# Four graph layers on one core: the chain from a third-layer unit to the last layer's products, re-cut

## The chip, the cores and the metric

One core of a Trainium2 chip. The metric is the device time of one execution in microseconds, the median over runs of the same kernel. An execution of the kernel before takes 1645.74 us (1645.39 to 1646.08 over 3 runs); the profiled one has a span of 1643.8 us.

## The reference, cut to what matters

Eight batch elements with 2048 nodes and 64 features pass through four layers. Each layer adds its input and is followed by a layer norm. All share one adjacency matrix.

```python
x = _layernorm(x + _L0_gnn_ref(x, adj, ...), axis=-1)   # attention, layer norm inside, elu
x = _layernorm(x + _L1_gnn_ref(x, ..., adj), axis=-1)   # attention, elu
x = _layernorm(x + _L2_gnn_ref(x, adj, ...), axis=-1)   # attention, relu
x = _layernorm(x + _L3_gnn_ref(x, ..., adj), axis=-1)   # below

# layer 2, the "third layer"
h = jnp.matmul(x, W)
e = leaky_relu(f1[:, :, None] + f2[:, None, :])         # f1, f2: h times the two halves of a
attention = softmax(where(adj > 0, e, NEG_BIG), axis=2)
out = relu(matmul(attention, h))

# layer 3, the last layer
feat = softplus(x * (INV_SQRT2 * w0) + b0)
scores = feat * wa + ba
attn = softmax(where(mask, scores[:, None, :, :], -1e9), axis=2)
out = einsum('bijd,bjd->bid', attn, feat)
```

In the last layer the score of a neighbour depends on the neighbour and the feature alone. So with v = exp(scores) the output of a node is the sum over its neighbours of feat*v divided by the sum of v: two products of the adjacency matrix with a 2048 x 64 matrix for each element. A node without neighbours gets the mean of feat.

## The kernel before, in words

**Units.** The first three layers are done in 24 units of (layer, element): elements 0 to 3 through layers 0 and 1, then 4 to 7 through both, then layer 2 for elements 0 to 7. A unit is a loop over 16 steps, one for each block of 128 neighbours (`attend`, L899). In layer 2 a step is: POOL clamps a 128x2048 tile w from a row that is spread over the partitions (`clamp`, two steps ahead), ACT takes the exponential of each half of it into a PSUM tile e (`exponential`, one step ahead), DVE multiplies each half by the adjacency matrix (`edge`, fp8) back into w, and PE multiplies w with x into two accumulator banks (four products in the program, eight in the profile).

**Streams.** All other work is written as generators that a list of streams (`Streams`, L1190) advances by one pause at each attention step: `yield n` means "go on n steps later". Every engine executes its queue in the order in which these steps put instructions there. So the number and the place of the pauses decide where in an engine's queue an operation stands. After a unit's 16th step a chain of streams is added: `finish` (L937: divide, residual, statistics, normalize), then `scores` for the next layer or, after layer 2, `l3_features`. `group` (L757) makes the row maxima that layer 2 needs for four elements at a time; it runs once after element 3 and once after element 7 of layer 1.

**Banks.** [...] two for the accumulators of the running unit, two "side" banks (`pm`), handed out by a counter `pm_slots`, and four more that the current layer uses in its own way (in layer 2, two tiles e of two banks each). `Banks.share()` (L120) takes one of the two side banks away for the last layer's products (`pl_slots`). It is called at the hand-over to the first unit of layer 2, although the products begin only when the first two elements are through it. With one side bank, `finish` and `transposed` fetch one bank at a time instead of two (`Banks.width`).

**The last layer.** Its products need more than bf16 precision, so each operand is cut into three bf16 pieces v0, v1, v2 that add up to the fp32 value. `l3_features` (L1048) does, for one element: softplus (Abs, Exp, Ln, Relu on ACT, an addition on DVE), the scores on POOL, the sum of the features (`fs`) on DVE, the exponential, feat*v, then the pieces: ACT casts to v0, POOL subtracts it from the fp32 value, ACT casts the rest to v1, POOL subtracts again into v2. In between PE turns `fs` into a mean over all nodes (`p_fm`, `q.fm`), on which the stream waits for a side bank. Two elements make a pair with shared piece tiles 128 x 16 x 256; there are four pairs, and all but the last share one set of piece tiles (`v_slots`), so a pair's pieces are made when the pair before has placed all its products. The products of a pair (`l3_products`, L1115) are 16 row blocks of 48 matmuls (16 neighbour blocks by three pieces, `edge` stationary, 256 columns moving), placed as half blocks of 24, one per attention step when pieces and a bank are there. ACT copies a row block out (`nd`), and for every two row blocks `l3_finish` (L1158) divides, adds, normalizes and stores. When the eight units of layer 2 are over, the streams run alone until everything is placed (`now[0]` is 3); products then use the banks of the tiles e, which are two row blocks.

The profile gives nearly every instruction the line L78, that of the recording helper, so its groups are told apart by tile names: `acc` and `w` are attention, `p_l` the last layer's products, `vf` the fp32 value, `v` the pieces, `nd` the copied products, `st`, `isw` and `sq` statistics.

Of the kernel before, what the change touches and what calls it, by code (L numbers as in the profile page):

```python
# [8 lines left out]
F32 = mybir.dt.float32  # L9
# [5 lines left out]
ALU = mybir.AluOpType  # L15
AX = mybir.AxisListType

P = 128
# [30 lines left out]
def gnn4_kernel(ctx: ExitStack, tc: tile.TileContext, t, out):  # L49
    nc = tc.nc  # L50
    x_in, adjT = t["x"], t["adjT"]
    B, N, F = x_in.shape
# [9 lines left out]
    small = ctx.enter_context(tc.tile_pool(name="small", bufs=2))  # L62
# [40 lines left out]
    pm_slots = Slots(2)  # L103

    class Banks:
# [4 lines left out]
        pool = None  # L110
# [9 lines left out]
        @classmethod  # L120
        def share(cls):

            cls.shared = True
            pm_slots.n -= 1

        @classmethod
        def width(cls):
# [6 lines left out]
    xT_slots, h_slots, sq_slots, e_slots, v_slots, pl_slots, oT_slots = (  # L134
        Slots(1) for _ in range(7)
    )
    vf_slots, nd_slots, o_slots, lo_slots = (Slots(2) for _ in range(4))

    pe, dve, act, pool = (InOrder(e) for e in (nc.tensor, nc.vector, nc.scalar, nc.gpsimd))

    def psum(name):
        return pm.tile([P, 512], F32, tag="pm", name=name)
# [10 lines left out]
    ones = consts.tile([P, P], F32, name="ones")  # L153
# [67 lines left out]
    p = psum("p_nodes")  # L221
# [137 lines left out]
    def softplus(f, y, src):  # L359

        act.activation(y, src, AF.Abs, scale=l3c[:, 0:1], bias=l3c[:, 1:2])
        yield 1
        act.activation(y, y, AF.Exp, scale=-1.0)
        yield 1
        act.activation(y, y, AF.Ln, bias=1.0)
        yield 1
        act.activation(f, src, AF.Relu, scale=l3c[:, 0:1], bias=l3c[:, 1:2])
        yield 1
        dve.tensor_tensor(f, f, y, ALU.add)
# [387 lines left out]
    def group(gi):  # L757
# [61 lines left out]
        yield 1  # L819

        am = small.tile([P, NB, K], F32, tag="am", name=f"am_{nm}", bufs=1)
        slots = pl_slots if Banks.shared else pm_slots
        yield from slots.take()
        Banks.busy += 1
        p = psum(f"p_lse_{nm}")
        for ib in range(K):
            for jb in range(K):
                pe.matmul(
                    p[:, NB * ib : NB * (ib + 1)],
                    lhsT=edge[:, jb, ib * P : (ib + 1) * P],  # L830
                    rhs=te[:, jb, :],
                    start=(jb == 0),
                    stop=(jb == K - 1),
                )
            if ib % 4 == 3 or (gi == 0 and ib % 2):
                yield 1 if gi else 2
        dve.tensor_scalar(
            am.rearrange("p b k -> p k b"),
# [98 lines left out]
    def finish(u):  # L937
        layer, b = u.layer, u.b
        yield from oT_slots.take()
        oT = tmp.tile([P, 2, 512], F32, tag="oT", name=f"oT_{u.n}")  # L940
        for c in range(2):
            act.copy(oT[:, c], u.acc[c])
        if layer == 0:
            hb = early.tile([P, K, F], F32, tag="hb", name=f"hb_{u.n}", bufs=1)
            for sl, y in V[0, b].parts:
                pool.tensor_tensor(
                    hb[:, :, sl], y, bc_k(gamma[:, sl], K, y.shape[2]), ALU.mult
                )
        yield 1
        yield from o_slots.take()  # L950
        o = tmp.tile([P, K, F], F32, tag="o", name=f"o_{u.n}", bufs=2)
        o5 = o.rearrange("p (c h s) f -> p c s h f", c=2, h=2)
        done = 0
        while done < 4:
            width = Banks.width()
            ps = []
            yield from pm_slots.take(width)
            for i in range(done, min(done + width, 4)):
                c, s0 = i // 2, 2 * (i % 2)
                p = psum(f"p_o_{u.n}_{c}_{s0}")  # L960
                for s in range(2):
                    k = s0 + s
                    pe.matmul(
                        p[:, s * 2 * F1 : (s + 1) * 2 * F1],
                        lhsT=oT[:, c, k * P : (k + 1) * P],
                        rhs=RH[layer].rearrange("p h f -> p (h f)"),
                        start=True,
                        stop=True,
                    )
                ps.append((c, s0, p))  # L970
            done += width
            if done >= 4:
                oT_slots.give()
            yield 2 if pairs and width == 2 else 1
            for c, s0, p in ps:
                p4 = p[:, : 4 * F1].rearrange("p (s h f) -> p s h f", s=2, h=2)
                den = small.tile([P, 2, 2], F32, tag="den", name=f"den_{u.n}_{c}_{s0}")
                dve.reciprocal(den, p4[:, :, :, F])
                if layer == 2:
                    dve.tensor_tensor(  # L980
                        o5[:, c, s0 : s0 + 2],
                        p4[:, :, :, :F],
                        den[:, :, :, None].to_broadcast([P, 2, 2, F]),
                        ALU.mult,
                    )
                    continue
                for s in range(2):
                    for h in range(2):
                        act.activation(
                            o5[:, c, s0 + s, h],  # L990
                            p4[:, s, h, :F],
                            AF.Copy,
                            scale=den[:, s, h : h + 1],
                        )
            pm_slots.give(width)
        if layer == 2:
            for sl, x in x_cur[b].parts:
                dve.scalar_tensor_tensor(o[:, :, sl], o[:, :, sl], 0.0, x, ALU.max, ALU.add)
            yield 1
        else:  # L1000
            yield 1
            if layer == 0:
                pool.tensor_tensor(o, o, hb, ALU.add)
                yield 2

            yield from e_slots.take()
            e = tmp.tile([P, K, F], F32, tag="e", name=f"eh_{u.n}")
            act.activation(e, o, AF.Relu, scale=-1.0)
            act.activation(e, e, AF.Exp, scale=-1.0)
            yield 1  # L1010
            for sl, x in x_cur[b].parts:
                pool.tensor_tensor(
                    e[:, :, sl], e[:, :, sl], x, ALU.add
                )
            act.activation(o, o, AF.Relu)
            yield 1
            pool.tensor_tensor(o, o, e, ALU.add)
            e_slots.give()
            yield 1
        nm, rs = yield from stats(o, K, f"x_{u.n}")  # L1020
        xn = Rows(x_cur[b].t, layer < 2)
        if layer == 2:
            dve.tensor_tensor(o, o, bc_f(rs), ALU.mult)
            dve.tensor_tensor(xn.v, o, bc_f(nm), ALU.add)
            yield 1
        else:
            yield 1
            for k in range(K):
                act.activation(
                    xn.block(k), o[:, k], AF.Identity, scale=rs[:, k : k + 1], bias=nm[:, k : k + 1]  # L1030
                )
                if k % K2 == K2 - 1:
                    yield 1
            xn.settle()
        o_slots.give()
        x_cur[b] = xn
        V[layer + 1, b] = xn
        yield 1


    class Pair:
# [2 lines left out]
    pairs = []  # L1044

    now = [0]

    def l3_features(b):  # L1048

# [12 lines left out]
        y = tmp.tile([P, K, F], F32, tag="e", name=f"sp_{n}")  # L1062
        yield from softplus(f, y, x_cur[b].v)
        e_slots.give()
        yield 1
        v = late.tile([P, K, 2, F], F32, tag="vf", name=f"vf_{n}", bufs=2)
        pool.tensor_tensor(v[:, :, 1], f, bc_k(wa), ALU.mult)
        pool.tensor_tensor(v[:, :, 1], v[:, :, 1], bc_k(l3off), ALU.add)
        fs = small.tile([P, F], F32, tag="fs", name=f"fs_{n}")
        dve.tensor_reduce(fs, f.rearrange("p k f -> p f k"), AX.X, ALU.add)  # L1070
        yield 3
        act.activation(v[:, :, 1], v[:, :, 1], AF.Exp)
        yield 1
        dve.tensor_tensor(v[:, :, 0], f, v[:, :, 1], ALU.mult)
# [19 lines left out]
                yield 1  # L1094
        act.copy(q.v[0][:, :, i], v)
        yield 1
        pool.tensor_tensor(v, v, q.v[0][:, :, i], ALU.subtract)
        yield from pm_slots.take()
        p = psum(f"p_fm_{n}")
        pe.matmul(p[:, :F], lhsT=ones, rhs=fs, start=True, stop=True)  # L1100
        yield 1

        q.fm[i] = small.tile([P, F], F32, tag="fm", name=f"fm_{n}", bufs=4)
        dve.tensor_scalar(q.fm[i], p[:, :F], 1.0 / N, -1.0, ALU.mult, ALU.add)
        pm_slots.give()
        act.copy(q.v[1][:, :, i], v)
        yield 1
        pool.tensor_tensor(q.v[2][:, :, i], v, q.v[1][:, :, i], ALU.subtract)
        vf_slots.give()
        yield 1  # L1110
        q.ready += 1
# [2 lines left out]

    def l3_products():  # L1115

        for m in range(B // 2):
            while len(pairs) <= m or pairs[m].ready < 2:
                yield 1
            q = pairs[m]  # L1120
            for ib in range(K):
# [143 lines left out]
    for n, (layer, b) in enumerate(todo):  # L1265
# [17 lines left out]
        def handover():  # L1283

            if not done or nxt is None or S[nxt].__dict__.get("begun"):
                return
            if in_psum(*nxt):
                if n == 0:
                    Banks.use("psR", 1)
                spread(*nxt)  # L1290
            elif nxt == (2, 0):
                Banks.use("psE", 2)
                Banks.share()
            S[nxt].begun = True
            first_exponentials()

# [546 lines left out]
```

## Time and profile before

| | us | share of the span |
|---|---|---|
| span | 1643.8 | |
| PE, matmuls | 1349.0 | 82% |
| DVE | 1301.1 | 79% |
| POOL | 823.7 | 50% |
| ACT | 802.8 | 49% |
| PE, products of the last layer (`p_l`, 3072) | 351.1 | |
| layer 2, units 0 to 7 | 838.1 to 1396.5 | 34% |
| after the last unit | 1396.5 to 1643.8 | 15% |

A row of groups gives the operation, the tiles written and read with their shapes, its count, then busy time, the mean of one in ns, and the idle time of the engine just before it with what ended it. A row of windows gives, for a stretch of time, how long each engine was busy and with how many instructions. The chain of waits is followed back from the last instruction: each line is a start, a length, and the engine and tile that the end of the program waited for at that time.

### The profile page before, as it was taken

What the parts mean: (1) busy time and instruction counts of PE and PEld (TensorE: products, weight loads), DVE (VectorE), ACT (ScalarE), POOL (GpSimd) and SP (SyncE); (2) the same over time, 40 slices, a digit from 0 to 9 for tenths busy, and PEclk for the clock granted to TensorE, in tenths of its full rate; (3) what the DMA queues carried; (4) which work ended last, traced back from release to release, by engine and by line L of the source; (5) the groups of instructions that cost most, each with busy time, mean ns of one, the idle gap of its engine ahead of it and who ended that gap; (6) DMA issues with size and microseconds to landing.
All of it is one profiled execution on the core that took longest, in us unless ns stands there. A gap on an engine that the chain in (4) does not pass through costs nothing.

```text
span 1643.8 us, 20952 instructions
## 1 busy us (share of the span) xinstructions
PE 1349.0 (82%) x8162; PEld 667.2 (41%) x8162; DVE 1301.1 (79%) x1334; ACT 802.8 (49%) x1635; POOL 823.7 (50%) x726
## 2 busy tenths in 40 slices
PE   3687879888888898888887676699896999587996
PEld 2222323333333343233322231165452545476885
DVE  4888877899887989898888878969897977738444
ACT  5234664443265443442378857676656664242111
POOL 2145353422222454321257748877789877546332
PEclk9999988899998999999999878899998999888998
DMA  8800000000000000000000000000010000000000
GB/s 329 215 5 1 1 2 1 1 2 1 1 1 2 1 2 2 2 1 26 26 1 26 26 1 27 0 26 8 30 33 7 4 4 11 10 4 14 11 14 19
DMA packets 42190, 36.86 MB, mean 22 GB/s; under 512 B 37509, under 2 KB 37813, under 8 KB 39906
## 3 DMA queue, kind: packets, MB, share of 16 engines
q1 hardware_dynamic: 41538, 34.26, 6.8%
q8 instruction: 66, 1.08, 0.3%
q10 hardware_dynamic: 544, 1.17, 0.2%
q14 instruction: 42, 0.34, 0.1%
HBM read 30.94 MB, written 4.45 MB: 22 GB/s over the span
## 4 chain that ended last, share of the span: by engine, by line
PE 31%; DVE 17%; ACT 7%; POOL 4%; issue 3%; POOLq 0%; DVEq 0%; ACTq 0%
PE p_l L78 18%; PE acc L78 11%; DVE w L78 10%; ACT e L78 3%; DVE o L78 2%; DVE st_x L78 2%; DVE x L78 1%; POOL v L78 1%; PE p_o L78 1%; ACT x L78 1%; POOL vf L78 1%; DVE f L78 1%; PE p_s L78 1%; POOL w L78 1%; POOL o L78 1%
## 5 line engine op out<-in xcount | busy, mean ns | idle before, releaser
L78 PE MATMUL acc<-w,pv 128*64 128x512 f32 x2048 | 525.4, 642 | 117.0 <-DVE w L78 95.1
L78 DVE SCALAR_TENSOR_TENSOR w<-r,se,edge 128x2048 f32<-128x2048 f32 x240 | 551.9, 2340 | 27.1 <-PE r L78 26.3
L78 PEld LDWEIGHTS <-edge 128*128 128x128 fp8e4 x3842 | 321.2, 99 | 153.1 <-issue 94.3
L78 PE MATMUL p_l<-v,edge 128*128 128x256 bf16 x3072 | 351.1, 275 | 37.4 <-ACT nd L78 13.1
L78 PE MATMUL acc<-w,x 128*64 128x512 f32 x1024 | 281.8, 667 | 87.4 <-DVE w L78 79.9
L78 ACT ACTIVATE e<-w,s_g 128x1024 f32<-128x1024 f32 x256 | 277.6, 1113 | 148.1 <-DVE w L78 103.7
L78 DVE TENSOR_TENSOR w<-e,edge 128x1024 f32<-128x1024 f32 x256 | 300.3, 1214 | 56.3 <-ACT e L78 54.2
L78 PEld LDWEIGHTS acc<-w,pv 128*64 128x64 f32 x2048 | 134.9, 143 | 401.6 <-issue 199.5
L78 POOL TENSOR_SCALAR w<-row,hi_g,lo_g 128x2048 f32<-128x2048 f32 x128 | 270.5, 2118 | 37.6 <-PE acc L78 33.4
L78 PEld LDWEIGHTS acc<-w,x 128*64 128x64 f32 x1024 | 64.0, 146 | 231.9 <-DVE w L78 154.7
L78 POOL TENSOR_TENSOR eh<-eh,x 128x1024 f32<-128x1024 f32 (+2 forms) x24 | 36.5, 1533 | 153.2 <-ACT eh L78 153.2
L78 ACT ACTIVATE nd<-p_l,empty 128x256 f32<-128x256 f32 x64 | 30.1, 470 | 158.8 <-PE p_l L78 158.8
L78 ACT ACTIVATE x<-o,st_x 128x64 f32<-128x64 f32 x256 | 87.4, 432 | 26.9 <-DVE st_x L78 26.9
L78 ACT COPY oT<-acc 128x512 f32<-128x512 f32 x48 | 25.7, 587 | 122.6 <-PE acc L78 122.5
L78 ACT ACTIVATE o<-p_o,den 128x64 f32<-128x64 f32 x256 | 56.2, 323 | 48.5 <-DVE den L78 48.4
L78 DVE RECIPROCAL den<-p_o 128x4 f32<-128x4 f32 x96 | 16.9, 179 | 73.5 <-PE p_o L78 59.5
L78 POOL TENSOR_TENSOR st_h<-isw_h,mhalf 128x16 f32<-128x16 f32 x8 | 23.6, 2956 | 99.2 <-DVE isw_h L78 94.9
L78 PEld LDWEIGHTS p_o<-rh,oT 128*128 128x128 f32 x384 | 51.2, 200 | 53.5 <-issue 32.0
L78 POOL TENSOR_TENSOR st_x<-isw_x,mhalf 128x16 f32<-128x16 f32 x24 | 70.5, 2936 | 2.0
L78 PE MATMUL p_o<-rh,oT 128*128 128x130 f32 x384 | 64.0, 302 | 7.9 <-ACT o L78 5.6
L78 POOL TENSOR_SCALAR isw<-isw 128x4 f32<-128x4 f32 x32 | 8.5, 265 | 122.6 <-DVE isw L78 122.5
L78 DVE TENSOR_REDUCE st<-sq 128x4 f32<-128x256 f32 x32 | 13.2, 414 | 70.4 <-ACT sq L78 70.3
(233 smaller groups left out, 1511.5 us busy)
## 6 DMA issues: line engine op xcount, KB each, us to landing
raw<-in_adjT_dram SPq DMA_DIRECT2D x8, 1024.0 KB
raw<-in_adjT_dram SPq DMA_DIRECT2D x16, 512.0 KB
row<-rows_d_g SPq DMA_DIRECT2D x8, 1024.0 KB
x<-in_x_dram SPq DMA_DIRECT2D x8, 512.0 KB
out_dram<-o SPq DMA_DIRECT2D x64, 64.0 KB
row<-row_d ACTq DMA_DIRECT2D x1, 1024.0 KB
row_d<-rT SPq DMA_DIRECT2D x15, 12.0 KB
row<-row_d SPq DMA_DIRECT2D x15, 12.0 KB
```

The costliest lines, as they stand in the source:

```text
L78: ins = f(*args, **kwargs)
```

## The change

It shortens the way from the end of a third-layer unit to the point where that element's pieces are ready, so that the last layer's products can start earlier. It has these parts:

- `Banks.share` is now a stream of its own that waits for a side bank, and the product stream calls it when the first pair is ready. Until then both side banks serve `finish`, `scores` and `group`. `group` therefore always takes a side bank, and places its matmuls in smaller portions (every second row block instead of every fourth).
- softplus is placed in two steps: Abs with Exp, Ln with Relu, instead of four. Two pauses at the end of `finish` in layer 2 and one in `l3_features` are gone.
- The mean over the nodes is a stream of its own (`l3_mean`), so that the pieces no longer wait for a side bank.
- The two subtractions for the pieces of odd elements are on DVE instead of POOL.

```diff
@@ class Banks
         def share(cls):
+            yield from pm_slots.take()
             cls.shared = True
-            pm_slots.n -= 1
@@ def softplus(f, y, src):
         act.activation(y, src, AF.Abs, scale=l3c[:, 0:1], bias=l3c[:, 1:2])
-        yield 1
         act.activation(y, y, AF.Exp, scale=-1.0)
         yield 1
         act.activation(y, y, AF.Ln, bias=1.0)
-        yield 1
         act.activation(f, src, AF.Relu, scale=l3c[:, 0:1], bias=l3c[:, 1:2])
         yield 1
         dve.tensor_tensor(f, f, y, ALU.add)
@@ def group(gi):
-        slots = pl_slots if Banks.shared else pm_slots
+        slots = pm_slots
...
-            if ib % 4 == 3 or (gi == 0 and ib % 2):
+            if ib % 2:
                 yield 1 if gi else 2
@@ def finish(u):
             dve.tensor_tensor(xn.v, o, bc_f(nm), ALU.add)
-            yield 1
...
         V[layer + 1, b] = xn
-        yield 1
+        if layer < 2:
+            yield 1
@@
+    def l3_mean(q, i, fs, n):
+
+        yield from pm_slots.take()
+        p = psum(f"p_fm_{n}")
+        pe.matmul(p[:, :F], lhsT=ones, rhs=fs, start=True, stop=True)
+        yield 1
+        q.fm[i] = small.tile([P, F], F32, tag="fm", name=f"fm_{n}", bufs=4)
+        dve.tensor_scalar(q.fm[i], p[:, :F], 1.0 / N, -1.0, ALU.mult, ALU.add)
+        pm_slots.give()
@@ def l3_features(b):
         e_slots.give()
-        yield 1
...
         dve.tensor_reduce(fs, f.rearrange("p k f -> p f k"), AX.X, ALU.add)
-        yield 3
+        bg.add(l3_mean(q, i, fs, n))
+        yield 2
         act.activation(v[:, :, 1], v[:, :, 1], AF.Exp)
...
         act.copy(q.v[0][:, :, i], v)
         yield 1
-        pool.tensor_tensor(v, v, q.v[0][:, :, i], ALU.subtract)
-        yield from pm_slots.take()
-        p = psum(f"p_fm_{n}")
-        pe.matmul(p[:, :F], lhsT=ones, rhs=fs, start=True, stop=True)
-        yield 1
-
-        q.fm[i] = small.tile([P, F], F32, tag="fm", name=f"fm_{n}", bufs=4)
-        dve.tensor_scalar(q.fm[i], p[:, :F], 1.0 / N, -1.0, ALU.mult, ALU.add)
-        pm_slots.give()
+        eng = dve if i else pool
+        eng.tensor_tensor(v, v, q.v[0][:, :, i], ALU.subtract)
+        yield 1
         act.copy(q.v[1][:, :, i], v)
         yield 1
-        pool.tensor_tensor(q.v[2][:, :, i], v, q.v[1][:, :, i], ALU.subtract)
+        eng.tensor_tensor(q.v[2][:, :, i], v, q.v[1][:, :, i], ALU.subtract)
@@ def l3_products():
+        while len(pairs) == 0 or pairs[0].ready < 2:
+            yield 1
+        yield from Banks.share()
         for m in range(B // 2):
-            while len(pairs) <= m or pairs[m].ready < 2:
+            while pairs[m].ready < 2:
                 yield 1
@@ the hand-over to layer 2
                 Banks.use("psE", 2)
-                Banks.share()
```

## The prediction

> **What bounds the kernel now.** I read the page first (busy shares, then the slices), then the windows of the third layer and of what follows it, then the chain of waits over the same stretch. From the page:
>
> ```profile
> PE 1349.0 (82%) x8162; PEld 667.2 (41%) x8162; DVE 1301.1 (79%) x1334; ACT 802.8 (49%) x1635; POOL 823.7 (50%) x726
> PE   3687879888888898888887676699896999587996
> DVE  4888877899887989898888878969897977738444
> POOL 2145353422222454321257748877789877546332
> ```
>
> No engine is full over the span, but from slice 27 (about 1080 us) PE stands at 9 with a hole at 5, 8 and 7 late. That is where the last layer's products run. The windows cut that part at the starts of third-layer units 3 to 7 (the first multiply of each on DVE), at the last product of unit 7 (1396.5), and at the pauses of PE after it:
>
> ```profile
> core 0: us, PE busy (x) PEld busy (x) DVE busy (x) ACT busy (x) POOL busy (x), PEclk, DMA share, GB/s
> 1023.70:1089.20 65.50, 51.43 (x252) 20.46 (x249) 55.52 (x54) 48.34 (x47) 48.79 (x21) 0.89 0.05 17
> 1089.20:1165.40 76.20, 75.94 (x531) 45.77 (x530) 59.59 (x72) 48.65 (x54) 59.73 (x50) 1.00 0.07 20
> 1165.40:1239.70 74.30, 68.74 (x447) 38.09 (x443) 66.36 (x79) 44.78 (x48) 65.90 (x57) 0.98 0.07 20
> 1239.70:1320.30 80.60, 66.91 (x406) 35.45 (x408) 67.30 (x70) 56.32 (x58) 72.52 (x48) 0.94 0.02 4
> 1320.30:1396.50 76.20, 72.51 (x471) 40.40 (x468) 63.67 (x73) 41.16 (x45) 59.06 (x58) 0.96 0.03 8
> 1396.50:1419.20 22.70, 22.70 (x209) 20.51 (x210) 13.59 (x32) 4.43 (x9) 4.96 (x10) 1.00 0.03 8
> 1419.20:1444.70 25.50, 1.21 (x9) 0.65 (x8) 22.20 (x21) 12.12 (x11) 23.41 (x11) 0.59 0.05 10
> 1444.70:1477.70 33.00, 32.97 (x288) 28.82 (x288) 6.66 (x9) 15.52 (x15) 12.27 (x6) 0.96 0.02 5
> 1477.70:1490.80 13.10, 0.00 (x0) 0.00 (x0) 12.76 (x12) 3.12 (x4) 10.26 (x13) 0.66 0.00 0
> 1490.80:1629.60 138.80, 138.78 (x1250) 123.24 (x1249) 70.94 (x137) 20.11 (x41) 51.87 (x81) 0.98 0.07 15
> 1629.60:1643.80 14.20, 0.03 (x1) 0.00 (x0) 6.33 (x16) 1.20 (x3) 4.54 (x8) 0.58 0.10 24
> ```
>
> The tail after 1396.5 is thus 22.7 + 25.5 + 33.0 + 13.1 + 138.8 + 14.2 = 247.3 us, and two of its pieces, 25.5 and 13.1, are PE doing nothing. The chain of waits names what fills the first one:
>
> ```profile
> 1418.86 3.05 POOL st_x L78
> 1421.93 4.03 DVE st_x L78
> ...
> 1427.13 4.96 DVE x L78
> ...
> 1436.40 8.23 POOL v L78 x2
> 1444.67 22.36 PE p_l L78 x190
> ```
>
> The pause ends with two POOL subtractions of 4.1 us each that make the third pieces (v2) of elements 4 and 5. The second pause (before 1490.8) is released by ACT's copy of a product bank, which stood behind the softplus and exponential of element 7.
>
> **What the Trainium skill says.** "SBUF — State Buffer", section "Who interferes with whom": a VectorE instruction with two SBUF inputs and a GpSimd instruction that reads SBUF exclude each other, and the later one blocks for the whole of the first. The trace agrees: the 128x16 st_x operation took 4.03 us and the x addition 4.96 while POOL's vf subtractions (4.1 us each) ran; the same addition on o took 1.21. "GPSIMD Engine Reference", section "3.1 Elementwise — side-by-side cycle accounting", gives an fp32 addition of 2048 elements as 4497 ns on GpSimd and 2293 on VectorE. The POOL rows here are 4246 and 4099 ns; DVE has no such row, its 1024-element addition is 1.21. I take 2.3 us for an odd piece on DVE; the bounds are 2.2 and, if it waits for a whole POOL instruction first, 6.4. "ScalarE: Activation LUTs", section "What ACT_TABLE_LOAD costs", puts a load at 1283 ns, which is the 1283 ns of this trace.
>
> **The change, part by part.**
>
> *Both side banks kept, softplus in two steps, fewer pauses, mean as its own stream.* These add no work; they change at which attention step an instruction is placed in its engine's queue. The order lists of the two kernels show it exactly. Products go in half blocks of 24 matmuls. Per third-layer unit 3, 4, 5, 6, 7 the kernel before places 6, 14, 12, 12, 12 of them (56), the changed one 10, 15, 11, 14, 14 (64). So 8 x 24 = 192 products leave the tail. They are all that pair 1 (elements 2 and 3) had left there; the changed kernel finishes that pair at step 13 of unit 7, so its piece buffers are free two steps before the tail, and both pairs that remain are 2 x 768 = 1536 products.
>
> *The attention units.* PE gets 8 x 2.73 = 21.8 us more (a half block is 2.73 in the chain). DVE gets four odd pieces of 2.3 (elements 1 and 3) = 9.2, and about 7 us of finishing for 2 more row groups (a reciprocal of 1.74, two reductions of 0.4, small operations). POOL loses four subtractions, 4 x 4.1 = 16.4, but gains finishing work too. With the median of its row for each instruction of the lists, and two table loads per softplus, the eight units hold PE 410 -> 431, DVE 478 -> 494, POOL 421 -> 418, ACT 400 -> 407 us. Now the sum, over stretches of so many steps, of the busiest engine: for 2 steps 596 -> 590, for 3 steps 568 -> 562, for 4 steps 549 -> 547, for 8 steps 516 -> 524, for whole units 497 -> 512. The units took 558 us before (838.1 to 1396.5), between the 3- and the 4-step sums. So the extra products fall largely where PE waited for DVE: 14 us idle in unit 3 and 13.7 in unit 6. From these sums the units become -6 to +15 longer. I choose +5: the 3- and 4-step sums say -6 to -2, but ACT now does Ln and Relu in one step (1.28 + 1.06 + 1.23 + 1.28, next to 2.23 of exponentials, is 7.1 us, where the longest such step was 5.9), and odd pieces can wait for a clamp of 2.1 us on POOL.
>
> *The tail.* T is the end of unit 7's products.
> 1. Pair 2's pieces. The last product of pair 1 now stands ahead of the last two groups of attention products (2 x 1.87, and 0.41 for the mean), so at T - 4.1. ACT: bank copy 0.47, two casts of 1.9, to T + 0.1. POOL subtracts element 4 from T - 1.8 to T + 2.3; DVE's element 5 is shut out until then, to T + 4.6. The second casts end at T + 6.5. On POOL the second subtraction stands behind four small products (1.75) and a power (1.04) that needs DVE's reductions, until T + 7.8; then 4.1 to T + 11.9, and DVE's, shut out again, to T + 14.2. Ahead of the products PE still has one group of p_o, which needs a side bank that DVE empties after these (0.87 + 0.18 + 0.42): T + 15.7, and 0.6 on PE. I take T + 17. Before, the same products began at T + 48.2.
> 2. 1536 products at 2.62/24 = 0.109 us: 167.6. The side matmuls among them are under 2 us.
> 3. Pauses: the mean of element 7 is still in PE's queue, behind the first half of pair 2's block 6, which PE reaches at about T + 49. Its input: x of element 7 comes at about T + 39 (the p_o evictions, 3 us of statistics, the power of 2.95, two additions), then ACT's Abs, Exp, table, Ln, Relu behind element 6's casts to T + 50, the DVE addition 1.2 and the sum 1.9: T + 53. So 4 us, and 2 for product banks that wait behind ACT's casts. The 13.1 us pause goes: the copy of that bank now stands ahead of element 7's exponential in ACT's queue.
> 4. The end, from the last product to the last output, is unchanged: 14.2.
>
> Sum: 17 + 167.6 + 6 + 14.2 = 204.8, against 247.3: -42.5. Costed at nothing: DVE's odd pieces of element 7, hidden by some 80 us of pair 2's products still to run; the earlier softplus of the constants, in layer 0, moved by two steps; the mean's scaling (0.2 us), beside products.
>
> **Forecast and rivals.**
> - *A, forecast (0.60)*: 1645.7 - 42.5 + 5 = 1608.
> - *B, the units pay for what they take (0.23)*: PE was 99% and 95% busy in units 4 and 7, so the 8 half blocks could cost all of their 21.8 us, and the odd pieces 4 more. 1645.7 - 42.5 + 26 = about 1630. Against it: of the eight net additions four fall in unit 3 and two in unit 6, where PE idled 14 us each.
> - *C, better than A (0.09)*: the units get 6 us shorter, as the 2- and 3-step sums say, and the pieces are done at T + 13: 1645.7 - 46 - 6 = 1594.
> - *D, slower (0.05)*: odd pieces at the front of DVE's queue hold up the multiplies each time POOL has the access, and the units take 22 + 9 = 31 us; in the tail the pieces merely wait for one another, both pauses stay, and only the 192 products leave (-21). 1645.7 + 31 - 21 = 1656. For it: DVE is at 84 to 89% in units 5, 6 and 7. Against it: the second pause comes from ACT's order, which the lists show changed.
> - *No change (0.03)*: B and D half each.
>
> **The numbers.** The time is A's. The range reaches down past C to 1590 and up past B to 1634; outside are D, no change and the edges of B and C. Faster is A + B + C = 0.92, same 0.03, slower 0.05.
>
> **What would show it.** Right: the products begin some 17 us after the last attention product, PE then runs without a pause above 5 us, the last product to the end is about 14 us, and units 0 to 7 together take 550 to 575 us. The first pause should end on a DVE or POOL v, with the DVE subtractions at 2.3 us or stretched to a POOL neighbour's end. Wrong: units 5 to 7 stretched with the multiplies waiting behind vf or v on DVE (B, D); a pause at the mean of element 6 or 7 of 10 us or more; the products starting after T + 25.

## The result, and the profile after

The changed kernel takes 1626.51 us (1624.74 to 1626.83), the kernel before 1645.57 beside it; the ratio is 0.9883, with a 95% interval of 0.9866 to 0.9900. The forecast was 1608 in a range of 1590 to 1634: the direction and the range held, and the gain is half of what was forecast, 19.1 us instead of 37.5.

The windows of the changed kernel, cut like those of before: units 0 to 7 of the third layer by the first multiply of each, the end of the last unit at 1416.6, then PE's pauses. Columns: the stretch, its length, then busy time with instructions for PE, PE loads, DVE, ACT and POOL, and the clock.

```profile
836.10:888.60 52.50, 41.13 (x184) 12.89 (x180) 41.61 (x43) 47.06 (x73) 40.71 (x22) 0.97 0.05 20
888.60:961.50 72.90, 50.08 (x303) 18.20 (x305) 61.08 (x75) 51.06 (x62) 41.43 (x21) 0.81 0.04 15
961.50:1030.50 69.00, 46.95 (x287) 14.91 (x287) 59.05 (x60) 47.33 (x45) 50.20 (x24) 0.85 0.04 16
1030.50:1100.50 70.00, 61.22 (x362) 30.75 (x362) 61.68 (x60) 49.70 (x49) 49.20 (x30) 0.93 0.04 16
1100.50:1177.20 76.70, 74.28 (x517) 44.22 (x516) 61.81 (x77) 48.55 (x54) 62.35 (x56) 1.00 0.07 22
1177.20:1264.40 87.20, 66.73 (x405) 35.15 (x407) 71.83 (x85) 54.72 (x55) 73.22 (x57) 0.90 0.06 17
1264.40:1343.70 79.30, 75.47 (x503) 42.61 (x500) 64.68 (x71) 48.27 (x52) 60.09 (x52) 0.98 0.03 6
1343.70:1416.60 72.90, 72.64 (x506) 43.55 (x503) 56.95 (x71) 43.70 (x48) 56.31 (x54) 1.00 0.04 8
1416.60:1432.70 16.10, 2.20 (x17) 1.96 (x14) 15.67 (x16) 6.93 (x8) 13.33 (x8) 0.65 0.00 1
1432.70:1460.90 28.20, 28.19 (x247) 24.70 (x246) 22.22 (x30) 12.06 (x13) 17.55 (x11) 0.96 0.05 10
1460.90:1471.30 10.40, 5.40 (x48) 4.59 (x47) 4.67 (x7) 9.11 (x11) 7.23 (x4) 1.00 0.00 0
1471.30:1609.70 138.40, 138.34 (x1250) 122.97 (x1250) 73.16 (x141) 20.57 (x42) 47.98 (x84) 0.99 0.07 15
1609.70:1624.90 15.20, 0.00 (x0) 0.00 (x0) 6.33 (x16) 1.18 (x3) 4.54 (x8) 0.60 0.10 23
```

The tail is 1624.9 - 1416.6 = 208.3 us, against 247.3: 39.0 gained. In the 25.5 us before pair 2 PE had paused for 24.3; now it is 13.2 and a short one of 0.7. The pause of 13.1 has become two of 1.2 and 3.8 within the 10.4 us stretch. So PE's pauses in the tail went from 37.4 to 18.9 us, 18.5 less, and the 192 products that left are another 20.9.

Units 0 to 2 of the kernel before:

```profile
838.10:887.70 49.60, 41.32 (x184) 12.86 (x180) 42.79 (x43) 45.27 (x65) 35.63 (x19) 0.97 0.06 22
887.70:952.60 64.90, 44.62 (x183) 13.58 (x179) 54.34 (x72) 51.81 (x69) 43.63 (x23) 0.89 0.04 17
952.60:1023.70 71.10, 49.53 (x401) 18.58 (x403) 57.26 (x62) 46.42 (x44) 50.61 (x22) 0.84 0.05 16
```

With these, the eight units take 580.5 us instead of 558.4: 22.1 given back. Where, by unit: +2.9, +8.0, -2.1, +4.5, +0.5, +12.9, -1.3, -3.3. The rest, 2.0 us, lies ahead of layer 2 (the first multiply at 836.1 instead of 838.1). In the profiles of this study that start moved between 834.2 and 841.3, also among kernels whose first two layers are the same, so below I compare units and tail, not ends.

The start of the tail on PE, in order of time (start, length, operation, and in brackets the idle time before and what ended it):

```profile
1412.63 3.65 PE L78 MATMUL acc<-w,x 128*64 128x512 f32 x16
1416.21 0.41 PE L78 MATMUL acc<-emptyT,mean 3*64 3x512 bf16 x4
1417.33 1.16 PE L78 MATMUL p_o<-rh,oT 128*128 128x130 f32 x8 [0.71 <-ACT oT L78]
1431.68 1.20 PE L78 MATMUL p_o<-rh,oT 128*128 128x130 f32 x4 [13.19 <-DVE st L78]
1432.67 4.02 PE L78 MATMUL p_l<-v,edge 128*128 128x256 bf16 x24
...
1471.31 0.43 PE L78 MATMUL p_fm<-fs,ones 128*128 128x64 f32 x2 [3.81 <-DVE fs L78]
1471.58 138.07 PE L78 MATMUL p_l<-v,edge 128*128 128x256 bf16 x1248
```

and the pieces on DVE, then on POOL:

```profile
1416.83 4.47 DVE L78 TENSOR_TENSOR vf<-vf,v 128x2048 f32<-128x2048 f32 x1 [6.94 <-ACT v L78]
...
1422.38 1.74 DVE L78 RECIPROCAL nd<-nd 128x256 f32<-128x256 f32 x1
1424.05 2.22 DVE L78 TENSOR_TENSOR v<-vf,v 128x2048 bf16<-128x2048 f32 x1
1426.19 4.26 DVE L78 TENSOR_TENSOR o<-nd 128x256 f32<-128x256 f32 x1
```

```profile
1415.07 4.07 POOL L78 TENSOR_TENSOR vf<-vf,v 128x2048 f32<-128x2048 f32 x1 [6.81 <-ACT v L78]
...
1424.27 5.90 POOL L78 TENSOR_TENSOR v<-vf,v 128x2048 bf16<-128x2048 f32 x1
```

The products of pair 2 begin 16.1 us after the last unit. Alone, DVE's odd piece takes 2.22 us; the first one took 4.47 because POOL was subtracting the even one until 1419.1, and the small product on o took 4.26 beside POOL's second subtraction, which ended at 1430.2. What ends PE's pause is neither: it is the bank of p_o, which DVE empties only after all these.

Where the units lose is best seen in the middle of unit 5, where PE has no products, since pair 0 is through and pair 1's pieces are being made. PE:

```profile
1213.91 1.94 PE L78 MATMUL acc<-w,x 128*64 128x512 f32 x8
1216.66 2.21 PE L78 MATMUL acc<-w,x 128*64 128x512 f32 x8 [0.81 <-DVE w L78]
1226.92 3.64 PE L78 MATMUL acc<-w,x 128*64 128x512 f32 x8 [8.05 <-DVE w L78]
1231.38 2.21 PE L78 MATMUL acc<-w,x 128*64 128x512 f32 x8 [0.82 <-DVE w L78]
1240.49 3.68 PE L78 MATMUL acc<-w,x 128*64 128x512 f32 x8 [6.90 <-DVE w L78]
```

and what stood ahead of those multiplies in DVE's queue:

```profile
1215.40 2.34 DVE L78 TENSOR_TENSOR w<-e,edge 128x1024 f32<-128x1024 f32 x2
1219.51 4.47 DVE L78 TENSOR_TENSOR vf<-vf,v 128x2048 f32<-128x2048 f32 x1 [1.78 <-ACT v L78]
1223.91 1.21 DVE L78 TENSOR_REDUCE st_x<-sq_x 128x16 f32<-128x1024 f32 x1
...
1232.80 2.29 DVE L78 TENSOR_TENSOR v<-vf,v 128x2048 bf16<-128x2048 f32 x1 [0.34 <-ACT v L78]
...
1235.10 1.22 DVE L78 TENSOR_TENSOR o<-o,st_x 128x1024 f32<-128x1024 f32 x1
1236.35 2.96 DVE L78 TENSOR_TENSOR x<-o,st_x 128x1024 f32<-128x1024 f32 x1
1239.23 2.34 DVE L78 TENSOR_TENSOR w<-e,edge 128x1024 f32<-128x1024 f32 x2
```

From these lines one would blame the odd pieces on DVE. The experiments decide otherwise. In the kernel before, the same pieces were made from 1234.9 to 1263.8, at the end of unit 5 and in unit 6; now it is 1215.8 to 1243.2, all in unit 5. PE stood idle for 10.9 us of the first stretch and for 16.7 of the second. So the gap came one unit earlier, and longer: PE's idle time went from 5.6 to 20.5 us in unit 5, and from 13.7 to 3.8 in unit 6.

### The profile page after: what moved, and what is told of

Read it like the earlier page. It is cut to its first block, busy times and chain, and to the rows that moved or that the text cites. A ratio compares the mean times of both kernels' runs of the same rounds, so it can differ in the third digit from the quotient of the medians.

```text
span 1624.9 us, 20941 instructions
## 1 busy us (share of the span) xinstructions
PE 1339.4 (82%) x8162; PEld 661.7 (41%) x8162; DVE 1302.9 (80%) x1334; ACT 803.8 (49%) x1635; POOL 804.4 (50%) x726
## 4 chain that ended last, share of the span: by engine, by line
PE 25%; DVE 19%; ACT 9%; POOL 5%; issue 3%; POOLq 0%; ACTq 0%; DVEq 0%
PE p_l L78 16%; DVE w L78 11%; PE acc L78 8%; ACT e L78 4%; DVE o L78 2%; DVE st_x L78 1%; ACT sp L78 1%; DVE vf L78 1%; POOL vf L78 1%; ACT x L78 1%; POOL w L78 1%; PE p_o L78 1%; ACT v L78 1%; POOL e L78 1%; DVE nd L78 1%
## 5 line engine op out<-in xcount | busy, mean ns | idle before, releaser
L78 PEld LDWEIGHTS acc<-w,pv 128*64 128x64 f32 x2048 | 133.7, 142 | 400.1 <-issue 196.0
L78 ACT ACTIVATE x<-o,st_x 128x64 f32<-128x64 f32 x256 | 87.4, 431 | 26.2 <-DVE st_x L78 26.2
L78 PE MATMUL p_o<-rh,oT 128*128 128x130 f32 x384 | 61.2, 297 | 23.4 <-DVE st L78 13.2
L78 DVE TENSOR_REDUCE st<-sq 128x4 f32<-128x256 f32 x32 | 13.2, 414 | 64.0 <-ACT sq L78 64.0
L78 POOL COPY x<-x 128x16 f32<-128x16 f32 x16 | 3.3, 204 | 120.3 <-ACT x L78 120.3
```

What stands on the lines that cost most here:

```text
L78: ins = f(*args, **kwargs)
```

## The experiments

The kernel before took a median of 1646.9 to 1647.3 us in the runs beside these. "Units" and "tail" are read from each profile as above; "half blocks" are the groups of 24 products left after the last unit, by the order lists.

| kernel | half blocks after the units | units | tail | sum | ratio to before (95%) |
|---|---|---|---|---|---|
| before | 72 | 558.4 | 247.3 | 805.7 | 1 |
| changed | 64 | 580.5 | 208.3 | 788.8 | 0.9883 (0.9866 to 0.9900) |
| odd_pool | 64 | 578.9 | 205.8 | 784.7 | 0.9879 (0.9863 to 0.9896) |
| odd_late | 64 | 579.2 | 206.6 | 785.8 | 0.9886 (0.9870 to 0.9903) |
| banks_before | 64 | 584.4 | 207.8 | 792.2 | 0.9886 (0.9867 to 0.9905) |
| softplus_four | 69 | 572.4 | 230.4 | 802.8 | 0.9986 (0.9979 to 0.9993) |
| mean_inline | 65 | 575.2 | 218.3 | 793.5 | 0.9913 (0.9895 to 0.9931) |
| pauses_before | 66 | 579.7 | 218.9 | 798.6 | 0.9939 (0.9914 to 0.9963) |
| odd_one | 64 | 577.2 | 206.5 | 783.7 | 0.9860 (0.9842 to 0.9877) |
| dve_345 | 64 | 577.3 | 203.9 | 781.2 | 0.9856 (0.9840 to 0.9872) |
| group_4 | 64 | 575.9 | 203.0 | 778.9 | 0.9846 (0.9823 to 0.9869) |
| group_1 | 64 | 576.2 | 205.2 | 781.4 | 0.9830 (0.9811 to 0.9848) |

**Odd pieces back on POOL**, for all elements or for 1 and 3 alone.

```diff
-        eng = dve if i else pool
+        eng = pool                                        # odd_pool
+        eng = dve if i and b >= B // 2 else pool          # odd_late
```

> The changed kernel with both subtractions of odd elements on POOL again; the products stand in the same steps (64 half blocks in the units, 64 after). Theory 1, the subtractions at the head of DVE's queue make the multiplies of unit 5 wait (4.5 us of vf plus 2.3 us of v in the stretch where PE stands for 8 and 7 us): unit 5 falls from 87.2 to 78 to 82, the eight units from 580.5 to 572 to 576, the first products of the tail move from 16.1 us after the last attention product to 19 to 23, and the total is 1620 to 1626. Theory 2, the pieces cost the same on either engine, and the units are longer because of what stands in them: the units stay within 3 us of 580.5, the tail takes 4 to 6 more, and the total is 1629 to 1633.

> The changed kernel with the subtractions of elements 1 and 3 on POOL and those of 5 and 7, which lie at the end and after the units, on DVE; the products stand in the same steps. Theory 1 (the head of DVE's queue): the units shrink by 4 to 9 us as without any odd piece on DVE, and the tail keeps its start at 16 us, so 1617 to 1623. Theory 2 (what stands in them): within 2.5 us of the changed kernel's 1626.5.

1627.77 and 1629.02 us. In both, unit 3 was 2.8 to 3.1 us shorter and unit 5 2.2 longer (89.4): theory 1 falls. Theory 2 has the units right, but not the tail: in odd_pool it is 2.5 us shorter, not 4 to 6 longer. Most of the products start 18.0 us after the last unit there instead of 16.1, but the later pauses are 2.4 instead of 5.0 and the end 13.8 instead of 15.2. In unit 5 the multiplies wait with the pieces on either engine. On POOL, odd_pool's trace shows a 128x16 operation on DVE (isw_x) at 3.98 us beside the second subtraction, with the multiplies behind it, and later a clamp that begins only at 1246.9, behind two subtractions of 8.1 us together. This part of the change moved nothing in the total that can be measured.

**Bank handling of before.** 

> The changed kernel with the bank handling of before (one side bank given away at the start of layer 2, group 1 in the other with portions of four row blocks). By the order lists not one product changes its step: 10, 15, 11, 14, 14 half blocks in units 3 to 7. Theory 3, both side banks crowd the side work of units 0 to 2 into fewer steps and this is what the 8.9 us there are: units 0 to 2 fall from 194.4 to 185 to 188 and the total is 1616 to 1620. Theory 4, these 8.9 us come from the features of elements 0 and 1 that the shorter chain brings into units 1 and 2: units 0 to 2 stay at 192 to 196 and the total is within 3 us of 1626.5.

```diff
-        while len(pairs) == 0 or pairs[0].ready < 2:
-            yield 1
-        yield from Banks.share()
...
                 Banks.use("psE", 2)
+                Banks.share()
```

(with the old slots and portions in `group`.) The time is 1630.95, with the same ratio as the changed kernel. Units 0 to 2 took 195.4, so theory 3 falls. Unit 0 alone went back to the length it had before; unit 1 got 3.4 shorter, units 2 and 3 got longer by 7.4 and 3.6. Theory 4 has the units right, though the median is 1.5 us above the total it allowed. Keeping both side banks is worth at most some 3 us.

**Softplus in four steps, the other pauses put back, the mean in its old place.** These move products.

> The changed kernel with softplus in four steps again. The order lists place 8, 16, 8, 12, 15 half blocks in units 3 to 7 and 69 after the last unit instead of 64. If the burst on ACT (Ln, Relu and two table loads in one step, 4.85 us) is what lengthens the units, they lose more than the 13.6 us of PE work that leaves them, 15 to 20, and the total is level with the changed kernel or faster (1621 to 1627). If the burst is hidden, the units lose 5 to 12 and the tail gains 13.6 plus pauses, and the total is 1630 to 1638.

> The changed kernel with the four other pauses of before put back (two at the end of the third layer's finish, one after softplus, three steps instead of two ahead of the exponential); softplus stays in two steps. The lists place 7, 15, 10, 16, 14 half blocks in the units and 66 after them. Theory 4 (the 8.9 us in units 0 to 2, where no product stands, are feature work of elements 0 and 1 that comes there earlier): units 0 to 2 fall from 194.4 to 186 to 190. Theory 5 (they come from the order within the steps, softplus above all): they stay at 193 or more. In both the tail gets longer by more than the 5.2 us of its two half blocks, by 8 to 15, since pair 1 now ends after the last unit: total 1628 to 1638.

> The changed kernel with the mean again inside the stream that makes the pieces, at the place it had, waiting for a side bank. The lists place 8, 16, 9, 15, 15 half blocks in the units and 65 after them: one more in the tail, and pair 2's pieces start behind it. If what counts is whether pair 1 ends before the last unit does (theory E), the units lose up to 3 us and the tail gains 8 to 20: 1632 to 1642. If only the number of products in the tail counts (theory N), 1625 to 1629.

```diff
+        yield 1                                           # softplus_four: after Abs and after Ln
...
-        yield 2                                           # pauses_before: ahead of the exponential;
+        yield 3                                           # and the three single pauses
...
-        bg.add(l3_mean(q, i, fs, n))                      # mean_inline
...
         eng.tensor_tensor(v, v, q.v[0][:, :, i], ALU.subtract)
-        yield 1
+        yield from l3_mean(q, i, fs, n)
```

1644.89, 1636.80 and 1632.29 us. Softplus in four steps alone takes back nearly the whole gain: its 5 more half blocks are 13.1 us of products (2.62 each), but its tail is 22.1 us longer. With 2 and 1 more half blocks the tails are 10.6 and 10.0 longer, of which 5.2 and 2.6 are products. So something beyond the count acts, 9.0, 5.4 and 7.4 us. Part of it stands at the start of pair 2: once the last half block of pair 1 lies after the last unit, the making of pair 2's pieces, which needs pair 1's tiles, starts later and no attention product is left to cover it. Most of pair 2's products start 33.0, 24.0 and 24.5 us after the last unit instead of 16.1; without pair 1's products ahead of them that is 3.8, 2.7 and 5.8 us later. In mean_inline two of PE's waits there end on the mean (fm), which the pieces wait for again, so this run does not separate the two. The rest lies later in the tail. PE in softplus_four:

```profile
1426.86 0.61 PE L78 MATMUL p_o<-rh,oT 128*128 128x130 f32 x4
1431.17 0.27 PE L78 MATMUL p_l<-v,edge 128*128 128x256 bf16 x1 [3.70 <-ACT v L78]
1437.59 0.37 PE L78 MATMUL p_l<-v,edge 128*128 128x256 bf16 x1 [6.15 <-ACT v L78]
1445.51 4.71 PE L78 MATMUL p_l<-v,edge 128*128 128x256 bf16 x23 [7.55 <-DVE isw_x L78]
...
1480.49 0.69 PE L78 MATMUL p_fm<-fs,ones 128*128 128x64 f32 x2 [11.88 <-DVE fs L78]
```

The three pauses before pair 2 are 17.4 us in all, with the first product of each piece in between, against 13.9 in the changed kernel. A fourth, at the mean of element 7, is 11.9 us, where the changed kernel has 3.8 and, for a product bank, 1.2. So most of the 9.0 us is here, not at the start of pair 2: on ACT, element 7's softplus steps take turns with element 6's casts (from 1463.8 to 1474.4), and DVE's addition behind them takes 3.98 us. No run isolates this pause. The expectation for a hidden burst had the loss of the units right, and its total of 1630 to 1638 was too low.

The units of softplus_four lost 8.1 us for 13.6 us of PE work less (5 x 2.73). Units 0 to 2 stood at 196.0 there and at 198.5 with the pauses put back, so theory 4 was not borne out either: no single part brings back the 185.6 us of before, and no run put two parts back together. In mean_inline the tail and the total came as theory E said, the total at its lower end; the units lost 5.3, more than its 3.

**How much of the units' 22 us is the price of products?** Both kernels with all but 2 of each row block's 48 matmuls left out inside the units, one run each.

```diff
                     for v in q.v:
+                        if not alone and not (
+                            jb in (0, K - 1) and v is q.v[0]
+                        ):
+                            continue
                         pe.matmul(
...
-                    bias=empty[:, ib : ib + 1],
+                    bias=empty[:, ib : ib + 1] if alone else ones[:, 0:1],
```

> The kernel before, with all products of the last layer that lie inside the units cut from 48 to 2 matmuls for each row block (it leaves out the rest of those sums; every other instruction keeps its step, and the tail is whole). 28 row blocks, 1344 products, leave some 1288 x 0.114 = 147 us of PE work out of units 3 to 7. Units 0 to 2 stay at 185.5. What units 3 to 7 (372.8 before) fall to is what the side work and the multiplies take alone: 310 to 335. To be set against thin_after.

> The changed kernel with the same cut: 32 row blocks inside the units keep 2 of 48 matmuls. Theory P, the longer units are the price of the 192 products put into them, nearly in full: the eight units take within 5 us of those of thin_before, since without products both hold the same work. Theory S, the units are longer because side work stands more densely and waits more (odd pieces, softplus in two steps, both banks): the eight units are 12 us or more above those of thin_before.

Units 0 to 2 and units 3 to 7, in the thinned kernel before and then in the thinned changed one:

```profile
840.20:1025.80 185.60, 135.60 (x764) 45.01 (x762) 154.32 (x173) 143.43 (x177) 129.67 (x64) 0.89 0.05 18
1025.80:1376.50 350.70, 236.27 (x812) 60.84 (x809) 314.06 (x343) 237.81 (x248) 306.67 (x233) 0.82 0.05 14
```

```profile
835.90:1030.10 194.20, 139.77 (x772) 46.79 (x768) 161.80 (x176) 145.34 (x178) 133.31 (x66) 0.86 0.05 17
1030.10:1384.80 354.70, 226.83 (x813) 57.87 (x813) 321.57 (x357) 242.45 (x256) 303.50 (x245) 0.85 0.05 14
```

With nearly all products left out the units take 536.3 and 548.9 us: a difference of 12.6. With them it is 22.1. So 12.6 us of what was given back is there without the products (theory S, just above its 12), 8.6 of it in units 0 to 2, and 9.5 is what the products add to the difference. There are 192 more of them, with a PE work of 21.8 us: a bit under half of it was paid (theory P falls in its strict form). Put the other way, the 56 half blocks of before cost the units 22.1 us for 147 us of PE work; the changed kernel's 64 cost 31.6.

Two things bound this reading. The 12.6 us is not waiting alone: the copies and the finishing of row blocks stay in the thinned kernels, for 32 row blocks in one and 28 in the other, and DVE is busy for 483.4 and 468.4 us in them, 15 more, blocked time included. And the attention products were slower in both: in units 3 to 7 one took 750 and 731 ns on average, against 648 and 642 in the whole kernels, where the granted clock was 0.95 and 0.96 instead of 0.82 and 0.85. PE's busy time in units 3 to 7 of the kernel before thus fell by 99 us, not by 147. So the products may cost more than 22.1 and 31.6; the difference of 9.5 is touched less, since both thinned kernels were slowed.

**Are the 8.6 us in units 0 to 2 meetings of work in one step?** Unit 1 of the changed kernel has one step of 11.2 us and one of 8.2. DVE in the first:

```profile
909.43 4.82 DVE L78 TENSOR_TENSOR w<-e,edge 128x1024 f32<-128x1024 f32 x4
917.25 0.35 DVE L78 TENSOR_REDUCE lc_g<-s 128x4 f32<-128x64 f32 x2 [3.01 <-ACT s L78]
917.51 1.48 DVE L78 SCALAR_TENSOR_TENSOR st_x<-st_x 128x16 f32<-128x16 f32 x1
918.91 1.21 DVE L78 TENSOR_TENSOR o<-o,st_x 128x1024 f32<-128x1024 f32 x1
920.16 2.96 DVE L78 TENSOR_TENSOR x<-o,st_x 128x1024 f32<-128x1024 f32 x1
```

DVE stands for 3.0 us at group 1's first reduction, which waits for ACT's copy of the scores, and then does element 0's normalization in the same step, before the next multiplies. Group 1 has time until unit 4, so it can begin later:

```diff
                 if layer == 1 and b % NB == NB - 1:
-                    end += [lambda b=b: group(b // NB)]
+                    end += [1 if b == B - 1 else 0, lambda b=b: group(b // NB)]    # group_1; 4 in group_4
```

(`chain` is changed to skip a pause of 0.) These two were built on dve_345, below.

> The same with group 1 begun one step later: its first reductions leave step 6, but its scalars meet element 0's exponential and pieces one step on. Theory 6: unit 1's 11.2 us step shrinks by about the 3 us that DVE waits there for ACT's copy of the scores, and units 1 and 2 take 138 to 141, the total 1621 to 1624. If DVE has that much work there: 140 to 143, within 2 us of 1624.4.

> The kernel with elements 3, 4 and 5 on DVE, and group 1 begun four steps later; by the lists the products keep their steps (10, 15, 11, 14, 14, and 64). Group 1's DVE work then no longer meets element 0's normalization (step 6 of unit 1, 11.2 us) and its softplus sum (step 9, 8.2 us). If such meetings in one step are what makes units 0 to 2 longer than before (Theory 6), units 1 and 2 fall from 141.8 to 135 to 139, the later units stay, and the total is 1617 to 1621. If DVE simply has that much work there, units 1 and 2 stay at 140 to 143 and the total within 2 us of 1624.4.

1618.16 and 1622.31 us. Units 1 and 2 took 138.0 and 138.5 instead of 141.8, and the 11.2 us step became 7.1 in both: theory 6 holds for these 3.5 us. Unit 3 gave 2.3 and 1.7 back. The totals missed what was expected, group_4's by 1.3 us above and group_1's by 2.8 below. Units and tail of group_1 sum to what dve_345 has; its lower time comes with a start of layer 2 at 834.2 instead of 840.1, which the edit doesn't touch. The profiles thus put the two and dve_345 within 2.5 us of each other.

**Better places for the odd pieces.**

```diff
-        eng = dve if i else pool
+        eng = dve if b == 3 else pool                     # odd_one
+        eng = dve if b in (3, 4, 5) else pool             # dve_345
```

> The changed kernel with the odd pieces on DVE for element 3 alone. With all odd pieces on POOL unit 3 was 2.8 us shorter, unit 5 was 2.2 longer and the tail 2.5 shorter; if these are additive by place, unit 3 takes 67.2, unit 5 87.2, the tail 205.8, and the total is 1619 to 1623. If the differences are only the scatter between runs of the same chip, within 2.5 us of the 1627.8 of all odd pieces on POOL.

> The changed kernel with the subtractions of elements 3, 4 and 5 on DVE, those of 1, 2, 6 and 7 on POOL; the products keep their steps. For pair 2 at the start of the tail four subtractions of 2.3 us then follow each other on one engine (9.2) where POOL and DVE shut each other out (4.1 + 2.3 twice, 12.8). If this chain sets the start of the products, they start 12 to 14 us after the last attention product instead of 16.1 and the total is 1618 to 1623. If the bank of p_o that DVE empties after them sets it, the start stays at 15 to 17 and the total within 2 us of the 1624.4 of the kernel with element 3 alone on DVE.

1624.39 and 1624.44 us. Odd_one has the predicted 67.2 and 87.2 us in units 3 and 5 and a tail of 206.5; its total lies between the two that were expected, with a late start of layer 2 (841.3). In dve_345 the products start 12.4 us after the last unit instead of 16.1, as expected where the two engines no longer shut each other out. DVE there:

```profile
1415.84 4.49 DVE L78 TENSOR_TENSOR vf<-vf,v 128x2048 f32<-128x2048 f32 x2 [5.14 <-ACT v L78]
...
1422.84 4.42 DVE L78 TENSOR_TENSOR v<-vf,v 128x2048 bf16<-128x2048 f32 x2
1427.17 0.42 DVE L78 TENSOR_TENSOR o<-nd 128x256 f32<-128x256 f32 x1
```

Two subtractions on DVE take the time in which the changed kernel did one behind POOL, and the product on o is back at 0.42 us from 4.26. The total of dve_345 did not follow: it is that of odd_one, as was expected if the start of the products did not move. The gain over odd_one, 2.6 us of tail, is in the profiles alone. The best of the study is group_1, 0.9830 (0.9811 to 0.9848) of before, against 0.9883 (0.9866 to 0.9900) for the change itself.

## Why the prediction was right, and where its size was off

1. *The tail: right.* Forecast 204.8, measured 208.3. The start at T + 17 was T + 16.1. The subtractions ended where the steps put them (POOL's first at T + 2.5, DVE's first at T + 4.7); only the order of the second ones was the other way, DVE first, and DVE's shut-out small product took the place of its shut-out subtraction. The mean of element 7 held PE for 3.8 us, forecast 4, at T + 51 to T + 55, forecast 49 to 53; the product banks 1.2, forecast 2. The second pause was gone, as the order lists said. From the first to the last product it was 177.0, forecast 175.6 with the side matmuls (under 2 us, which the forecast's sum of 204.8 left out); the end 15.2 instead of 14.2.
2. *The attention units: the term that was mis-sized.* "From these sums the units become -6 to +15 longer. I choose +5": measured +22.1, beyond both ends, and 580.5 us is outside the 550 to 575 that were to show the forecast right. The added work was sized well: in the units DVE is busy 11.9 us more (forecast 16), ACT 7.6 more (7), POOL 2.4 less (3), PE 17.5 more (21). What failed is the step "so the extra products fall largely where PE waited for DVE", and with it the choice of the 3- and 4-step sums because they lay nearest to the measured 558 us. These sums take the busiest engine of each stretch, so they credit PE's gaps with products. The gaps in units 3 and 6 did shrink, from 27.8 us of idle PE to 12.6. But new ones came, 14.9 us in unit 5, to which the making of pair 1's pieces had moved, and 6.1 in units 0 to 2. Over all eight units PE stood idle for 87.4 us before and for 92.0 after. The thinned kernels put 12.6 of the 22.1 us down to what is there without the products, and 9.5 to the products; of the 12.6, waits at the head of DVE's queue are shown for 3.3 to 3.8 only (group_4 and group_1). The whole-unit sums, which only add up work, had +15: nearer in number, but without these waits, so not for the right reason. The ACT burst named as the reason for +5 was not isolated: softplus_four shed 8.1 us in the units, but 5 half blocks with it.
3. *The odd pieces.* Their 2.3 us and the shutting-out were right (2.2 alone, 4.47 behind POOL). That they would cost the units something against POOL was wrong: 1.6 us at most. In unit 5 the multiplies did wait behind vf and v on DVE, which was named as a sign of B or D; odd_pool shows that they wait as long without that.
4. *The rivals.* What came is nearer in number to B (units +26, tail -42.5, about 1630) than to the forecast, and the range held because it was drawn past B. B's reasons are not borne out: the 8 half blocks did not cost all of their 21.8 us, the odd pieces cost almost nothing, and over half of the loss is there without the products, which neither account has. D's second half, that both pauses stay, did not happen. The sum of the forecast, -42.5 + 5, reads -39.0 + 22.1 - 2.0 in the measurement.

What stays open: what makes up the rest of the 12.6 us. The meeting of group 1 with element 0 is 3.3 to 3.8 of it. Both side banks are 3 in unit 0, but the run without them gave more back in units 2 and 3. In units 3 to 7 of the thinned kernels the differences are +4.4, +3.0, +11.0, -6.6 and -7.8 us; those of units 5 and 6 go with the making of pair 1's pieces, which moved from one to the other. No run separated these from each other.

## What to carry to other kernels

When work moves from an idle tail into a loop, price the tail by its chain and the loop by what is already queued there: here the chain came out within 2%, while the loop took back more than half of the gain. Work given to an engine that has gaps isn't free: here the gaps of two units shrank around 8 more half blocks, and the gap of unit 6 came back longer in unit 5. Because each engine takes its queue in order, a wait at its head holds what stands behind it, as the 3.0 us on DVE in unit 1 did. A run with the added work thinned out separates its price from that of the rearrangement; look at the granted clock and at the length of the other instructions in that run too, since thinning changed both. Where buffers are handed from one round to the next, look for the round that ends just before or just after a boundary: two more pauses in softplus moved 5 half blocks over it, and that was worth 14 us by the profiles and 17 by the times.

## What was not expected

- One half block more after the last unit came with a tail longer by 10.0 us (mean_inline), four times its products' 2.6.
- Leaving out 147 us of PE products inside the units of before made the units only 22.1 us shorter, 15%; part of the rest went into attention products that took 750 ns instead of 648. The 21.8 us more of the changed kernel account for 9.5, 44%.
- A subtraction of 2048 elements took 4.1 us on POOL and 2.2 on DVE, but sharing pair 2's four subtractions between the two engines was slower than giving all four to DVE, which started the products 3.7 us earlier.
